# Layer 1's normalization: channel sums added on GpSimd, steps begun a quarter earlier, one turned tile in another PSUM pool

## The chip, the cores and the metric

The kernel runs on one core of one Trainium2 chip. The time is device microseconds of one execution, as the median of several runs. A core has five engines with a queue each: TensorE (PE, matmuls; PEld are its weight loads), VectorE (DVE), ScalarE (ACT), GpSimd (POOL) and SyncE (SP, which here issues most DMAs). Matmul results land in PSUM and are moved to SBUF by VectorE or ScalarE.

## The reference

Four layers follow each other on an image batch of 8 x 56 x 56 x 192; each adds a block to its input after a group normalization. The change is inside layer 1, a shifted window attention:

```python
mu = jnp.mean(x, axis=-1, keepdims=True)
var = jnp.var(x, axis=-1, keepdims=True)
x = (x - mu) * jax.lax.rsqrt(var + EPS) * gamma + beta      # over the 192 channels of a token
sx = jnp.roll(x, shift=(-3, -3), axis=(1, 2))
win = ...                                                   # 8 x 8 windows of 7 x 7 = 49 tokens
qkv = (win @ w_qkv + b_qkv)...
attn = softmax(q * scale @ k.T + bias + mask)               # 6 heads
out = (attn @ v) @ w_proj + b_proj
```

What is changed is how the two sums over channels come about, of x and of x squared for every token, from which mean and variance follow.

## The kernel before

Channels lie on partitions: an image is a tile of 128 partitions (two halves of the rows, 64 channels each) by 3 channel blocks by pixels. Layer 1 goes through 8 images (b), and each image in four **quarters** (g): 7 rows of each half, 16 windows. A quarter is one turn of the loop over g, and its work is written out by hand in one string, `plan`, whose letters are taken in turn. VectorE, ScalarE, GpSimd and TensorE keep exactly that order (`manual_schedule`); an engine's instruction waits in its queue until the one ahead of it is done.

- X: exponentials of the scores (ScalarE, L928), Y: their sums and reciprocals (VectorE, L933, L934) and the product with them (GpSimd, L935); one X and one Y for each half, called X0, X1, Y0, Y1 below.
- T: the shares turned by TensorE in three tiles of 128 x 512 for each half (L956), copied to SBUF by ScalarE (first and third, L961) and VectorE (second, L963).
- P: shares times values (L971), with two PSUM tiles, and the copies of the result (L980, L981).
- R: the output projection (L990, L997), added to the image by VectorE (L1004). G: statistics for layer 2 (L1007).
- Q (three times) and V (twice): queries, keys and values of the next quarter (L886, L901); ScalarE evacuates Q's first half (L890) behind the X ahead of it, and the first values (L906).
- E: scores of the next quarter (L916), the mask added and the maximum taken by VectorE (L921, L923), the maximum subtracted by GpSimd (L924); E0 and E1 for the halves.
- N: one step of the generator `layer1_norm` for the next image. There are 13 in a quarter, called N1 to N13 below.

```python
plan = "X Q N Y V N X G Q N Y N T T T P N V N N T T T P G Q N R N E N R N G E N R N".split()
```

`layer1_norm` clears the gaps of the window tile `xr` (L782, L783), then, for each of four tiles of 16 windows, copies the image scaled by the group normalization into window order with eight GpSimd instructions, two a step (`windows`, L805), and squares it with two ScalarE instructions (`squares`, L812). For two tiles at a time a burst of matmuls with a matrix of 1/192 sums x (L844) and its squares (L848) over channels into one PSUM tile of the pool `mm`; ScalarE squares the mean (L855), VectorE subtracts (L859). After both halves come the floor (L818), Ln (L820) and Exp (L822), `finish`, and for each tile `scaled`: a matmul that spreads the factor over partitions (L827) and two VectorE products (L832). That is 33 steps, begun in quarter 0 of an image for the next image; `run(steps)` ahead of quarter 3 takes whatever is left, since quarter 3 is the first that reads the next image's `xr`. The windows' copies fall in N1 to N8 and the squares in N9 to N12 of quarters 0 and 1, each burst of sums in N13, and `finish` and `scaled` in N1 to N7 of quarter 2. Quarter 3 has no step.

PSUM: the pool `mm` has three banks, used by Q, V, R's first half, the sums, L827 and the third turned tile; the pool `et` has two, for the first two turned tiles, P and R's second half.

Image data for image b + 2 is loaded by SyncE in quarters 1 to 3 of image b (L761): rows of quarter 0 first, of quarters 1 and 2 next, of quarter 3 last.

Of the kernel before, what the change touches and what calls it, by code (L numbers as in the profile page):

```python
# [10 lines left out]
F32 = mybir.dt.float32  # L11
AF = mybir.ActivationFunctionType
ALU = mybir.AluOpType
# [76 lines left out]
def kernel(ctx: ExitStack, tc: tile.TileContext, a: dict, out: bass.AP):  # L90
# [681 lines left out]
    def in_pairs(z):  # L772
        return z.rearrange("p (k z t) -> p k z t", z=2, t=WN)

    def layer1_norm(b, x, pool, psum, consts, first=False):


        ones32, sel = consts[4:]
        xr = pool.tile([128, XR], F32, name="xr")
        blocks = xr[:, 0:12 * GW].rearrange("p (g j n) -> p g j n", j=3, g=4)  # L780
        pads = xr[:, 0:12 * GW].rearrange("p (a n) -> p a n", n=PW)
        nc.gpsimd.memset(pads[:, :, WN:64], 0.0)  # L782
        nc.gpsimd.memset(xr[:, 12 * GW:], 0.0)  # L783
        rs = pool.tile([128, TT], F32, name="rs1", bufs=1)
        msq = pool.tile([128, TT], F32, name="msq", bufs=1)
        yield xr
        sc, sh = scsh1[:, 0, b:b + 1], scsh1[:, 1, b:b + 1]

        def windows(g):

            xg = x[:, :, 7 * g:7 * g + 7]
            copies = []
            for j in range(3):
                for z, nw in ((0, 4), (1, 3)):
                    dst = blocks[:, g, j].rearrange("p (k n) -> p k n", n=PW)[:, 0:nw, 64 * z:64 * z + WN]
                    src = xg[:, j, :, 3 + 28 * z:3 + 28 * z + 7 * nw].rearrange("p i (w j) -> p w i j", j=7)
                    copies.append((dst.rearrange("p k (i j) -> p k i j", j=7), src))
            last = blocks[:, g, :, 3 * PW + 64:3 * PW + 64 + WN].rearrange("p c (i j) -> p c i j", j=7)
            copies += [(last[:, :, :, 0:4], xg[:, :, :, 52:56]), (last[:, :, :, 4:7], xg[:, :, :, 0:3])]
            for n, (dst, src) in enumerate(copies):  # L800
                if first and n % 3 == 1:
                    nc.scalar.activation(dst, src, AF.Identity, bias=sh, scale=sc)
                else:
                    eng = nc.vector if first and n % 3 == 2 else nc.gpsimd
                    eng.tensor_scalar(dst, src, sc, sh, ALU.mult, ALU.add)  # L805
                if n % 2:
                    yield

        def squares(g, sq):
            for z in range(2):  # L810
                src = blocks[:, g].rearrange("p c (k n) -> p c k n", n=PW)[:, :, :, 64 * z:64 * z + WN]
                nc.scalar.activation(  # L812
                    sq[:, z].rearrange("p c (k t) -> p c k t", t=WN), src, AF.Square
                )
                yield

        def finish(rows):
            nc.vector.tensor_scalar(rs[rows], rs[rows], 0.0, 1e-5, ALU.max, ALU.add)  # L818
            yield
            nc.scalar.activation(rs[rows], rs[rows], AF.Ln)  # L820
            yield
            nc.scalar.activation(rs[rows], rs[rows], AF.Exp, scale=-0.5)  # L822
            yield

        def scaled(g):
            bp = psum.tile([128, 512], F32, name="rstd", tag="mm", bufs=3)[:, 0:TT]
            nc.tensor.matmul(bp, sel[32 * g:32 * g + 32], rs[32 * g:32 * g + 32], start=True, stop=True)  # L827
            for z in range(2):
                xs = blocks[:, g].rearrange("p c (k n) -> p c k n", n=PW)[:, :, :, 64 * z:64 * z + WN]
                by = bp[:, 4 * WN * z:4 * WN * (z + 1)].rearrange("p (k t) -> p k t", t=WN)  # L830
                by = by.unsqueeze(1).to_broadcast([128, 3, 4, WN])
                nc.vector.tensor_tensor(xs, xs, by, ALU.mult)  # L832

        for g0, n in ((0, 1), (1, 1), (2, 2)) if first else ((0, 2), (2, 2)):
            sqs = []
            for g in range(g0, g0 + n):
                yield from windows(g)
            for g in range(g0, g0 + n):
                sqs.append(pool.tile([128, 2, 3, 4 * WN], F32, name="sq", bufs=2))
                yield from squares(g, sqs[-1])  # L840
            ps = psum.tile([128, 512], F32, name="stat", tag="mm", bufs=3)
            for j in range(3):
                for k in range(n):
                    nc.tensor.matmul(  # L844
                        in_pairs(ps[32 * k:32 * k + 32, 0:TT]), ones32, in_slots(xr, (3 * (g0 + k) + j) * GW),
                        start=(j == 0), stop=(j == 2),
                    )
                    nc.tensor.matmul(  # L848
                        ps[64 + 32 * k:96 + 32 * k, 0:TT].rearrange("p (z n) -> p z n", z=2), ones32, sqs[k][:, :, j],
                        start=(j == 0), stop=(j == 2),  # L850
                    )
            rows = slice(64, 64 + 32 * n)
            for z in range(2):
                src = in_pairs(ps[0:32 * n, 0:TT])[:, :, z]
                nc.scalar.activation(  # L855
                    msq[rows, 4 * WN * z:4 * WN * (z + 1)].rearrange("p (k t) -> p k t", t=WN), src, AF.Square
                )
            to = slice(32 * g0, 32 * (g0 + n))
            nc.vector.tensor_tensor(rs[to], ps[rows, 0:TT], msq[rows], ALU.subtract)  # L859
            yield  # L860
            if first:
                yield from finish(to)
                for g in range(g0, g0 + n):
                    scaled(g)
                    yield
        if first:
            return
        yield from finish(slice(0, 128))
        for g in range(4):
            scaled(g)  # L870
            yield
# [70 lines left out]
    def layer1_mix(g, x, v, pool, psum, es, consts, st):  # L942
# [6 lines left out]
        def turn(s, i):  # L949

            e, et = es[g % 2][s], ets[s]
            tag, bufs = ("mm", 3) if i == 2 else ("et", 2)
            tp = psum.tile([128, 512], F32, name="et_ps", tag=tag, bufs=bufs)
            for k in range(4):
                at = 8 * i + 2 * k
                nc.tensor.transpose(  # L956
                    tp[:, 128 * k:128 * k + 128], e[:, at:at + 2].rearrange("p a b -> p (a b)"), ident
                )
            dst = et[:, 4 * i:4 * i + 4].rearrange("p a b -> p (a b)")
            if i % 2 == 0:  # L960
                nc.scalar.copy(dst, tp)  # L961
            else:
                nc.vector.tensor_copy(dst, tp)  # L963
# [509 lines left out]
    with ExitStack() as st:  # L1473
# [37 lines left out]
        ))  # L1511
        last = slice(nimg - 1, nimg)
        gn, stats = [], []
        for b in range(nimg):
            gn.append(pool.tile([128, 3, NTH, 6], F32, name="gh_st"))
            steps = iter(())
            if b + 1 < nimg:
                steps = layer1_norm(b + 1, x[b + 1], pool, psum, consts)
                xr.append(next(steps))
            for g in range(4):  # L1520
                if g == 1 and b + 2 < nimg:
                    x.append(layer1_image(xpool))
                if g and b + 2 < nimg:
                    for piece in ((), (0,), (1, 2), (3,))[g]:
                        rolled(x1[b + 2], x[b + 2], piece, False)
                if g == 1 and b == 0:
                    run(gn_finish(mv1[:, last], scsh1[:, 0, last], scsh1[:, 1, last], pool, psum, "mm"))
                if g == 1 and b:
                    gn_aggregate(gn[b - 1], mv2[:, b - 1])
                if g == 1 and b == nimg - 1:  # L1530
                    run(gn_finish(mv2[:, 0:b], scsh2[:, 0, 0:b], scsh2[:, 1, 0:b], pool, psum, "mm"))
                if g == 3:
                    run(steps)
                parts, now = layer1_mix(g, x[b], values, pool, psum, es, consts, gn[b])
                parts.update(softmax, G=stats)
                if g < 3 or b + 1 < nimg:
                    values, of_next, softmax = layer1_scores((g + 1) % 4, xr[b + (g == 3)], pool, psum, S, es, consts)
                    parts.update(of_next)
                for kind in plan:
                    if kind == "N":  # L1540
                        next(steps, None)
                    elif parts.get(kind):
                        parts[kind].pop(0)()
                stats = now
                rolled(x2[b], x[b], g, True)
# [231 lines left out]
```

## Time and profile before

| | us |
|---|---|
| median of 3 runs | 5501.04 (5497.55 to 5502.83) |
| the profiled execution | 5505.7, of which the span 5503.9 |
| layer 1's loop, from the first X0 to the last | 924.4 (2001.3 to 2925.7 of the span) |
| of it busy: TensorE | 839.1 |
| VectorE | 620.0 |
| ScalarE | 392.0 |
| GpSimd | 379.3 |

The page gives the span, busy times by engine and groups of instructions. A timeline line gives start, length, engine, line, operation, operands and a count; in square brackets stands how long the engine was idle before it and which engine, tile and line ended that. A window line gives, for a stretch of the span, the busy time of each engine (with instruction counts), the share of TensorE's full clock that was granted (PEclk), and DMA traffic. TensorE works a float32 matmul in two passes, which the profile counts as two records.

### The profile page before, as it was taken

What the parts mean: (1) busy time and instruction counts of PE and PEld (TensorE: products, weight loads), DVE (VectorE), ACT (ScalarE), POOL (GpSimd) and SP (SyncE); (2) the same over time, 40 slices, a digit from 0 to 9 for tenths busy, and PEclk for the clock granted to TensorE, in tenths of its full rate; (3) what the DMA queues carried; (4) which work ended last, traced back from release to release, by engine and by line L of the source; (5) the groups of instructions that cost most, each with busy time, mean ns of one, the idle gap of its engine ahead of it and who ended that gap; (6) DMA issues with size and microseconds to landing.
All of it is one profiled execution on the core that took longest, in us unless ns stands there. A gap on an engine that the chain in (4) does not pass through costs nothing. (4 is left out here: it accounts for less than half of the span.)

```text
span 5503.9 us, 113538 instructions
## 1 busy us (share of the span) xinstructions
PE 4998.8 (91%) x49428; PEld 3379.9 (61%) x49428; DVE 3053.1 (55%) x4273; ACT 2311.1 (42%) x3109; POOL 1877.9 (34%) x1583
## 2 busy tenths in 40 slices
PE   7999969999999979999987989998798787999999
PEld 6778866666666645666665757775344586444444
DVE  4555533555555456666666868888777214343331
ACT  3444435555555434444441025554576302333333
POOL 5555555555555434344431023333011101001000
PEclk9999989999999989999998999999899898999999
DMA  5989896777777623223225757675777696212211
GB/s 148 234 222 232 222 269 261 272 273 275 277 276 272 201 68 85 77 81 86 82 59 156 270 214 235 230 237 188 182 218 220 241 340 235 65 61 87 70 40 27
DMA packets 533335, 1002.87 MB, mean 182 GB/s; under 512 B 256104, under 2 KB 467812, under 8 KB 501460
## 3 DMA queue, kind: packets, MB, share of 16 engines
q1 hardware_dynamic: 519984, 945.58, 53.5%
q0 software_dynamic: 8576, 40.69, 2.3%
q10 hardware_dynamic: 4276, 9.32, 0.6%
q8 instruction: 389, 6.37, 0.5%
q14 instruction: 110, 0.90, 0.1%
HBM read 665.22 MB, written 346.75 MB: 184 GB/s over the span
## 5 line engine op out<-in xcount | busy, mean ns | idle before, releaser
L465 POOL COPY lc<-lt 128x896 f32<-128x896 f32 (+1 forms) x320 | 616.4, 1934 | 513.9 <-PE op L473 490.7
L432 PE MATMUL qv<-w_qv_sb,x 64*112 64x256 f32 (+1 forms) x5376 | 692.0, 410 | 24.0 <-DVE act L438 20.1
L432 PEld LDWEIGHTS qv<-w_qv_sb,x 64*112 64x112 f32 x5376 | 592.5, 176 | 112.5 <-DVE act L438 32.2
L438 DVE TENSOR_TENSOR act<-qv,b_qv 112x640 f32<-112x640 f32 x448 | 318.7, 752 | 325.4 <-PE qv L432 238.5
L442 ACT ACTIVATE act<-act 112x640 f32<-112x640 f32 x448 | 300.3, 683 | 414.3 <-DVE act L438 403.7
L408 POOL TENSOR_TENSOR qv<-act 112x320 f32<-112x320 f32 x448 | 346.5, 799 | 288.9 <-ACT act L442 193.6
L473 PEld LDWEIGHTS op<-rc,lc 128*56 128x56 f32 x9216 | 329.6, 135 | 124.2 <-issue 65.9
L1366 PE MATMUL ph<-y,w_sb 64*128 64x392 f32 x2304 | 398.9, 499 | 6.5 <-ACT hid L1370 6.5
L473 PE MATMUL op<-rc,lc 128*56 128x56 f32 x9216 | 354.5, 221 | 55.1 <-ACT rc L465 38.2
L1377 PE MATMUL po<-hid,w_sb 128*64 128x392 f32 x2304 | 386.3, 494 | 0.0
L1384 DVE TENSOR_TENSOR x<-x,z 128x392 f32<-128x392 f32 x96 | 72.8, 759 | 520.3 <-ACT z L1382 520.3
L1097 PE MATMUL cv<-zc,wt 128*128 128x224 f32 x1536 | 312.8, 355 | 24.9 <-DMA zc<-pd 24.2
L1097 PEld LDWEIGHTS cv<-zc,wt 128*128 128x128 f32 x1536 | 290.3, 189 | 68.3 <-issue 53.1
L1366 PEld LDWEIGHTS ph<-y,w_sb 64*128 64x128 f32 x2304 | 220.7, 189 | 176.5 <-issue 26.5
L506 PE MATMUL y<-pp,w_o_sb 128*64 128x392 f32 x1536 | 309.0, 499 | 5.8 <-DVE pp L500 5.8
L1112 POOL TENSOR_TENSOR rows<-rows,loc 128x896 f32<-128x896 f32 x96 | 223.3, 2326 | 261.9 <-ACT rows L1108 204.6
L483 PE MATMUL pj<-xn,w_p_sb 64*128 64x392 f32 x1536 | 289.1, 509 | 19.7 <-ACT pp L490 18.1
L924 POOL TENSOR_TENSOR e<-e,mx 128x1176 f32<-128x1176 f32 x64 | 140.2, 2190 | 462.6 <-DVE mx L923 398.3
L465 ACT COPY rc<-rt 128x896 f32<-128x896 f32 (+1 forms) x160 | 279.9, 1749 | 40.0 <-DMA rt<-right 40.0
L1377 PEld LDWEIGHTS po<-hid,w_sb 128*64 128x64 f32 x2304 | 162.7, 137 | 213.8 <-issue 213.8
L500 DVE TENSOR_TENSOR pp<-pp,ot 128x784 f32<-128x784 f32 x128 | 124.1, 970 | 292.6 <-PE ot L495 239.9
L1115 DVE TENSOR_TENSOR_SCAN sums<-dec,rows 64x896 f32<-64x896 f32 x96 | 278.5, 2901 | 1.3
(252 smaller groups left out, 9194.8 us busy)
## 6 DMA issues: line engine op xcount, KB each, us to landing
lt<-left SPq DMA_DIRECT2D x72, 1792.0 KB
rt<-right SPq DMA_DIRECT2D x72, 1792.0 KB
left<-qv SPq DMA_DIRECT2D x224, 252.0 KB
right<-qv SPq DMA_DIRECT2D x96, 504.0 KB
wt<-in_band_dram SPq DMA_DIRECT2D x23, 2048.0 KB
zc<-pd SPq DMA_DIRECT2D x187, 232.0 KB
pd<-pt SPq DMA_DIRECT2D x7, 5568.0 KB
bm<-bmask SPq DMA_DIRECT2D x64, 588.0 KB
```

Of the source, the lines that this page charges most:

```text
L408: nc.gpsimd.tensor_tensor(qv[:, s, s0:s1, k], *(acts[s][:, which, 0:n].rearrange("p (s d) -> p s d", d=64) for which in range(2)), ALU.mult,)
L432: nc.tensor.matmul(ps[s][:, which, 0:n], x[64 * s:64 * s + 64, j, bass.ts(i, 2 * W)], w_qv[64 * s:64 * s + 64, j, which, 64 * s0:64 * s1], ...
L438: nc.vector.tensor_tensor(acts[s][:, :, 0:n], ps[s][:, :, 0:n], b_qv[:, :, 64 * s0:64 * s1], ALU.add)
L442: nc.scalar.activation(acts[s][:, :, 0:n], acts[s][:, :, 0:n], AF.Silu)
L465: copy(c[:, 0:nu], raw.rearrange("p (w u d) -> p u d w", u=nu, d=64 // nu)[:, :, d0:d0 + 8])
L473: nc.tensor.matmul(op[64 * u:64 * u + W, i, :], lc[:, u, i], rc[:, u, i], start=True, stop=True)
L483: nc.tensor.matmul(ps[:, s, 0:TT], w_p[64 * s:64 * s + 64, j, 128 * c:128 * c + 128], xn[64 * s:64 * s + 64, j, bass.ts(t, TT)], start=(j ...
L506: nc.tensor.matmul(y[64 * s:64 * s + 64], w_o[:, 2 * g + u, 64 * j:64 * j + 64], pp[:, u, s], start=(u == 0), stop=(u == 1),)
L1097: nc.tensor.matmul(dst, wt[:, c4 + i, 128 * q:128 * q + 128], zc[:, :, c4 + i, q:q + NPAIR], start=(q == 0), stop=(q == 1),)
L1115: nc.vector.tensor_tensor_scan(_reversed(sums[0:64]), d[0:64], _reversed(rows[0:64]), 0.0, ALU.mult, ALU.add)
L1366: nc.tensor.matmul(ps[:, s, 0:TT], w0[64 * s:64 * s + 64, j, m * 128:(m + 1) * 128], y[64 * s:64 * s + 64, j, ts], start=(j == 0), stop=(j ...
L1377: nc.tensor.matmul(ps[64 * s:64 * s + 64], w1[:, m, 64 * j:64 * j + 64], hid[:, m, s], start=(m == 0), stop=(m == 5),)
```

## The change

In `layer1_norm`, for all images but the first, GpSimd adds the three channel blocks of x (tile `xs`, two additions for each of the four tiles) and of the squares (in place in `sq`, two additions), so that one matmul instead of three sums each of them. Empty steps (`yield`) are put in. The generator then has 45 steps. Each image's steps begin in quarter 3 of the image before the one in which they began so far; for image 1 they begin where they did. In `turn` the second turned tile takes a bank of `mm` in place of one of `et`. In the changed kernel the lines behind `layer1_norm` stand 34 lower (X is L962, Q L920, V L935, T L990, P L1005), and the additions are L882, L883 and L887, the sums L892 and L895.

```diff
-        for g0, n in ((0, 1), (1, 1), (2, 2)) if first else ((0, 2), (2, 2)):
...
+        def variance(ps, g0, n):
             rows = slice(64, 64 + 32 * n)
...
+        if first:
+            for g0, n in ((0, 1), (1, 1), (2, 2)):
...
             return
+
+        for g0 in (0, 2):
+            tiles = []
+            for g in (g0, g0 + 1):
+                sq = pool.tile([128, 2, 3, 4 * WN], F32, name="sq", bufs=2)
+                xs = pool.tile([128, 4, 2, WN], F32, name="xs", bufs=2)
+                tiles.append((xs, sq))
+                yield from windows(g)
+                nc.gpsimd.tensor_tensor(xs, in_slots(xr, 3 * g * GW), in_slots(xr, (3 * g + 1) * GW), ALU.add)
+                nc.gpsimd.tensor_tensor(xs, xs, in_slots(xr, (3 * g + 2) * GW), ALU.add)
+                yield from squares(g, sq)
+                yield
+                for j in (1, 2):
+                    nc.gpsimd.tensor_tensor(sq[:, :, 0], sq[:, :, 0], sq[:, :, j], ALU.add)
+                yield
+            yield
+            ps = stat()
+            for k, (xs, sq) in enumerate(tiles):
+                nc.tensor.matmul(
+                    ps[32 * k:32 * k + 32, 0:TT], ones32, xs.rearrange("p k z t -> p (k z t)"), start=True, stop=True
+                )
+                nc.tensor.matmul(
+                    halves(ps[64 + 32 * k:96 + 32 * k, 0:TT]), ones32, sq[:, :, 0], start=True, stop=True
+                )
+            variance(ps, g0, 2)
+            yield
         yield from finish(slice(0, 128))
+        yield
+        yield
         for g in range(4):
             scaled(g)
             yield
...
-            tag, bufs = ("mm", 3) if i == 2 else ("et", 2)
+            tag, bufs = ("mm", 3) if i else ("et", 2)
...
+        def normalize(b):
+            if b >= nimg:
+                return iter(())
+            steps = layer1_norm(b, x[b], pool, psum, consts)
+            xr.append(next(steps))
+            return steps
+
+        steps = normalize(1)
         for b in range(nimg):
             gn.append(pool.tile([128, 3, NTH, 6], F32, name="gh_st"))
-            steps = iter(())
-            if b + 1 < nimg:
-                steps = layer1_norm(b + 1, x[b + 1], pool, psum, consts)
-                xr.append(next(steps))
...
                 if g == 3:
                     run(steps)
+                    steps = normalize(b + 2)
```

The steps fall as follows, for images 2 to 7. Quarter 3: copies of tile 0 (N1 to N4), its additions and squares (N5, N6, N8), copies of tile 1 (N9 to N12), its first additions and first square (N13). Quarter 0: its second square and last additions (N1, N3), the sums of tiles 0 and 1 (N5), copies of tile 2 (N6 to N9), its additions and squares (N10, N11, N13). Quarter 1: the same for tile 3 in N1 to N8, the sums of tiles 2 and 3 (N10), `finish` (N11 to N13). Quarter 2: `scaled` (N3 to N6).

More of the change, by code (lines that the diff above doesn't have):

```diff
@@ L832, in scaled @@
                 nc.vector.tensor_tensor(xs, xs, by, ALU.mult)
-        for g0, n in ((0, 1), (1, 1), (2, 2)) if first else ((0, 2), (2, 2)):
[L835 to L851, printed above, removed]
+        def variance(ps, g0, n):
             rows = slice(64, 64 + 32 * n)
@@ L859, in layer1_norm @@
             nc.vector.tensor_tensor(rs[to], ps[rows, 0:TT], msq[rows], ALU.subtract)
-            yield
-            if first:
+            return to
+        stat = lambda: psum.tile([128, 512], F32, name="stat", tag="mm", bufs=3)
+        halves = lambda z: z.rearrange("p (z n) -> p z n", z=2)
+        if first:
+            for g0, n in ((0, 1), (1, 1), (2, 2)):
+                sqs = []
+                for g in range(g0, g0 + n):
+                    yield from windows(g)
+                for g in range(g0, g0 + n):
+                    sqs.append(pool.tile([128, 2, 3, 4 * WN], F32, name="sq", bufs=2))
+                    yield from squares(g, sqs[-1])
+                ps = stat()
+                for j in range(3):
+                    for k in range(n):
+                        nc.tensor.matmul(
+                            in_pairs(ps[32 * k:32 * k + 32, 0:TT]), ones32, in_slots(xr, (3 * (g0 + k) + j) * GW),
+                            start=(j == 0), stop=(j == 2),
+                        )
+                        nc.tensor.matmul(
+                            halves(ps[64 + 32 * k:96 + 32 * k, 0:TT]), ones32, sqs[k][:, :, j],
+                            start=(j == 0), stop=(j == 2),
+                        )
+                to = variance(ps, g0, n)
+                yield
                 yield from finish(to)
@@ L865, in layer1_norm @@
                     yield
-        if first:
             return
+        for g0 in (0, 2):
[4 more added lines that the diff above has]
+                tiles.append((xs, sq))
+                yield from windows(g)
+                nc.gpsimd.tensor_tensor(xs, in_slots(xr, 3 * g * GW), in_slots(xr, (3 * g + 1) * GW), ALU.add)
[6 more added lines that the diff above has]
+            yield
+            ps = stat()
+            for k, (xs, sq) in enumerate(tiles):
+                nc.tensor.matmul(
+                    ps[32 * k:32 * k + 32, 0:TT], ones32, xs.rearrange("p k z t -> p (k z t)"), start=True, stop=True
+                )
+                nc.tensor.matmul(
+                    halves(ps[64 + 32 * k:96 + 32 * k, 0:TT]), ones32, sq[:, :, 0], start=True, stop=True
+                )
+            variance(ps, g0, 2)
+            yield
         yield from finish(slice(0, 128))
+        yield
+        yield
         for g in range(4):
```

## The prediction

> **What bounds the kernel now.** Section 1 of the page has TensorE busy 91%. Then the busy time by window, over quarters 0 to 3 of image b = 4, which the others repeat:
>
> ```profile
> core 0: us, PE busy (x) PEld busy (x) DVE busy (x) ACT busy (x) POOL busy (x), PEclk, DMA share, GB/s
> 2486.10:2514.20 28.10, 26.26 (x564) 17.35 (x560) 19.69 (x34) 14.08 (x24) 16.91 (x22) 1.00 0.28 77
> 2514.20:2542.70 28.50, 26.90 (x565) 17.52 (x564) 19.33 (x34) 14.03 (x25) 16.26 (x20) 1.00 0.59 144
> 2542.70:2576.60 33.90, 29.90 (x555) 19.86 (x556) 23.53 (x41) 12.04 (x20) 8.76 (x4) 0.95 0.18 54
> 2576.60:2602.70 26.10, 24.09 (x542) 16.84 (x540) 17.76 (x31) 10.98 (x18) 8.75 (x4) 1.00 0.25 71
> ```
>
> TensorE sets the pace, and quarter 2, with `finish` and `scaled`, costs 7.8 us over quarter 3. TensorE's timeline shows what stops it (two lines of quarter 2, then quarter 3):
>
> ```profile
> 2552.28 0.92 PE L827 MATMUL rstd<-rs,sel 32*128 32x392 f32 x2 [2.19 <-ACT rs L822]
> 2553.13 2.34 PE L956 MATMUL et_ps<-ident,e 128*128 128x128 f32 x12
> ...
> 2575.48 2.25 PE L886 MATMUL qk_ps<-xr,wg 64*128 64x392 f32 x12
> 2578.36 2.32 PE L901 MATMUL v_ps<-wg,xr 64*128 64x192 f32 x24 [0.62 <-DVE x L1004]
> 2580.41 2.97 PE L886 MATMUL qk_ps<-xr,wg 64*128 64x392 f32 x12
> 2583.31 1.53 PE L956 MATMUL et_ps<-ident,e 128*128 128x128 f32 x12
> 2585.63 0.27 PE L971 MATMUL po<-et,v 49*32 49x49 f32 x2 [0.80 <-ACT et L961]
> 2586.26 1.20 PE L971 MATMUL po<-et,v 49*32 49x49 f32 x94 [0.36 <-DVE et L963]
> ```
>
> I count from the quarter's first Q (2575.48 = 0): T starts at 7.83. See the wait of 2.19 for Exp, and that T then takes 2.34, not 1.53. GpSimd and ScalarE at the edge to the next quarter (Q at 2601.64):
>
> ```profile
> 2581.05 2.19 POOL L935 TENSOR_TENSOR e<-e,sm 128x1176 f32<-128x1176 f32 x1 [0.74 <-DVE sm L934]
> 2585.81 2.19 POOL L935 TENSOR_TENSOR e<-e,sm 128x1176 f32<-128x1176 f32 x1 [2.57 <-DVE sm L934]
> 2600.52 2.19 POOL L924 TENSOR_TENSOR e<-e,mx 128x1176 f32<-128x1176 f32 x1 [12.53 <-DVE mx L923]
> 2604.55 2.19 POOL L924 TENSOR_TENSOR e<-e,mx 128x1176 f32<-128x1176 f32 x1 [1.83 <-DVE mx L923]
> ```
>
> ```profile
> 2602.75 1.21 ACT L928 ACTIVATE e<-e 128x1176 f32<-128x1176 f32 x1 [6.32 <-POOL e L924]
> 2603.97 0.59 ACT L890 ACTIVATE qk<-qk_ps,bq 128x392 f32<-128x392 f32 x1
> ```
>
> Y0's product ends at 7.76, just when T can start: GpSimd has no slack there. X0 starts as E0's subtraction ends (2602.71), and Q's evacuation stands right behind X0. Prices, by line and shape:
>
> ```profile
> L805 POOL TENSOR_SCALAR xr<-x,scsh 128x196 f32<-128x196 f32 x83 | 43.1, 519 | 0.4
> L812 ACT ACTIVATE sq<-xr 128x588 f32<-128x588 f32 x56 | 34.8, 692 | 0.3
> L832 DVE TENSOR_TENSOR xr<-xr,rstd 128x588 f32<-128x588 f32 x60 | 45.1, 765 | 14.0 <-PE rstd L827 12.7
> ```
>
> [...] 2.19 us idle were enough for half clock in quarter 2 (PEclk 0.95, T 0.8 us longer). [...] the sums' four strips start within 20 ns of each other and come again every 0.33 us. [...]
>
> **The change part by part.**
>
> *Sums.* A burst held TensorE from 2511.42 to 2513.54, 2.1 us for 24 passes in six groups of four. Eight passes are two groups, 0.36 + 0.33, with the turn-over 0.8 us. 14 bursts save 18 us, all on TensorE's path.
>
> *Additions.* 16 an image of 392 elements. Nearest row L924: 1.86 ns an element, 0.73 us; dearest, L408 (865 ns for 320), 1.06. I take 0.85, 1.7 for a pair.
>
> *Loads.* SyncE's order does not change. The copies' rows were issued a quarter or more ahead, and landings take 5.2 to 9.5 us: nothing waits. The clearing of `xr` waits for the last Q of quarter 2, long done.
>
> *Quarter 3 (so far empty).* Clearing (0.83) and N1's copies (1.05) now stand ahead of Y0 on GpSimd, as in quarter 0 so far, where T waited 1.00. GpSimd: E1's subtraction ends 4.8, Y0 6.7 to 8.9, N2 and N3 to 11.0, Y1 to 13.2, N4 to 14.1. The square in N5 waits for N4's copies, and in the built order ScalarE's copies of V and of the second T stand behind it: square 14.8, V 15.3, second square 16.0, T's copy 16.6. The second P starts at 16.6, not 15.5. Quarter 27.1 after 26.2: **+0.9**.
>
> *Quarter 0.* The first square of tile 1 (N13 of quarter 3) stands ahead of X0 on ScalarE and waits for N12's copies. These stand behind E1's subtraction on GpSimd. From Q: E0's subtraction ends 1.1, N10 and N11 3.2, E1's subtraction 5.4, N12 6.25, square 7.0, X0 8.2, Q's evacuation 8.8 (so far 2.9). The second Q takes that bank in the built order, and its other half waits for the first V's copy, behind the copy of k (0.84) and another square (0.69): 10.8, so far 5.65. TensorE loses 5.2; nothing behind is early enough to take it up. With the sums (0.8) and 0.2 from the turned tile: 26.2 + 5.2 + 0.8 - 0.2 = 32.0 after 28.1. An idle time twice that of quarter 2 brings half clock; one slice of 3.4 us costs 1.7. **+5.6**.
>
> *Quarter 1.* N13's additions (1.7) and N1's copies put Y0 at 7.7 to 9.9; T waits 2.1, of which P's waits give back 1.1. Then the squares hold the second P as in quarter 3. 28.8 with the sums, after 28.5: **+0.3**.
>
> *Quarter 2.* Exp is long done: 2.19 gone. Next is VectorE: `scaled` 0 and 1, four products of 0.765, now stand ahead of T1's copy, with Y1's reduction between. That copy ends at 14.2, P's second third waits 2.7, the second P ends at 22.4, so far 24.1, and the tail is 0.3 shorter: **-2.0**. Half clock as before.
>
> *Turned tile.* P's second matmul no longer waits for L963's copy (0.36), but passes that had waited ran faster (94 in 1.20, unhindered 96 in 1.6): 0.2 a quarter. The third tile now needs Q's bank, free by then.
>
> *Image 1.* Three quarters only, so four `scaled` come in one piece ahead of quarter 3: 3.2 of matmuls, 6.1 of VectorE, Q's banks held until products 1 and 2 are done: V some 7.9 late. By quarter: -1.2, +5.4, -4.7, +7.7 = +7.2.
>
> Sum: 6 x (0.9 + 5.6 + 0.3 - 2.0) = 28.8, image 1 +7.2, five last quarters -1.0: **+35 us**, span 5539. The profiled execution is 4.7 over the median; I add 35 to the median: **5536**.
>
> **The rivals.**
> 1. *Faster:* the end of `finish` decides. Place: quarter 2. If T1's copy is not late and no half clock follows, quarter 2 falls from its mean of 35.1 (six images; 33.4 to 38.4) to 31.5, -3.6; with X0 gated by N11 alone (3.4 us earlier, 1.8 lost, no half clock) quarter 0 is +0.5. 6 x (0.9 + 0.5 + 0.3 - 3.6) = -11, image 1 +2, last -1: 5491. It decides once quarter 0 loses less than about 2.4. For it: the 2.19 is the longest regular stall. Against: the built order has the square's wait on the last copy.
> 2. *Much slower:* additions at 1.06 and half clock for two slices in quarter 0 and one in quarter 1 (T's wait of 2.1 is near the 2.19): +4.2 an image and +3: 5564. For: half clock lasted 17 us once (quarter 2 of image 3, PEclk 0.78).
> 3. *The early start does not come about* (a late load or a held buffer stalls GpSimd, and with it the softmax). Each us is lost in full, 7 times; 2 us give 5550. Against: the landings above.
>
> **How the numbers follow.** Forecast 0.70 (own range 5513 to 5554: half clock absent or double, additions at both ends), rival 1 0.14, rival 2 0.13, rival 3 0.03. The range 5500 to 5565 leaves out most of rival 1 and the far end of rival 2. The 0.2% that a measurement of this kernel can tell is 11 us. Faster 0.11 from rival 1; same 0.07 from its slow end and the forecast's low end; slower 0.82.
>
> **What would show it.** ScalarE's first exponential of each quarter 0 some 6 us behind E0's subtraction, with the square ending just before it and GpSimd named as its releaser; TensorE idle some 5 us ahead of the second Q there, PEclk below 1; bursts of 0.8 us; no 2.19 ahead of L827; a wait of P for VectorE in quarter 2; additions of 0.73 to 1.06. Wrong, if X0 follows E0 within 3 us in quarter 0, or if quarter 2 falls to 31 or less.

## The result, and the profile after

| | before | after |
|---|---|---|
| median of the runs, us | 5501.5 (6 runs) | 5542.2 (6 runs) |
| ratio to before, with its 95% interval | | 1.0071 (1.0058 to 1.0084) |
| span of the profiled execution, us | 5503.9 | 5540.5 |
| layer 1's loop, from the first Q of image 0's quarter 1 to that of image 7's quarter 2, us | 858.7 | 909.2 |
| GpSimd busy in the loop, us | 379 | 485 |

The change makes the kernel 0.7% slower, 40.7 us by the medians, where 35 were forecast. In the profiled executions the loop is 50.5 us longer. Outside it, where nearly all of the code is the same, this execution was some 14 us shorter: its first stage alone ended 8.8 us sooner, before anything that was changed. Such differences come without a cause in the change: over the profiled executions of this text's eleven kernels the time outside the loop lies between 4631 and 4646 us. So the forecast's total fits better than its terms, and the terms are what the experiments are about.

A quarter is measured from its first Q to the next one's. The four quarters that the prediction worked through, of the same image, in the view of windows of the kernel after (start and end, length, then the busy time of TensorE, its weight loads, VectorE, ScalarE and GpSimd with instruction counts, the granted share of TensorE's clock, and DMA):

```profile
2602.77:2629.70 26.93, 24.34 (x544) 16.90 (x541) 18.33 (x32) 12.06 (x20) 18.39 (x21) 1.00 0.25 71
2629.70:2661.83 32.13, 27.34 (x552) 17.94 (x548) 18.29 (x33) 13.78 (x24) 18.76 (x23) 0.95 0.19 55
2661.83:2690.59 28.76, 24.75 (x552) 16.87 (x548) 19.05 (x34) 12.62 (x22) 20.99 (x21) 1.00 0.60 154
2690.59:2729.17 38.58, 33.36 (x552) 22.82 (x548) 25.55 (x42) 11.90 (x20) 8.32 (x5) 0.82 0.16 48
```

These are quarters 3, 0, 1 and 2. Quarter 0 and quarter 2 are the long ones, and they are the two with a clock below 1. The means over images 1 to 6 (quarter 3: 1 to 5), with the size that the prediction gave each:

| quarter | before | after | measured | predicted |
|---|---|---|---|---|
| 3 | 26.4 | 26.9 | +0.4 | +0.9 |
| 0 | 28.5 | 32.5 | +3.9 | +5.6 |
| 1 | 28.6 | 29.1 | +0.6 | +0.3 |
| 2 | 34.9 | 37.9 | **+3.0** | **-2.0** |

Image 0's four quarters, in the first three of which image 1 is normalized, rose by 5.4 us together (predicted 7.2): by 0.5, 0.6, 3.6 and 0.7 us (predicted -1.2, +5.4, -4.7 and +7.7).

Quarter 0 goes in its mechanism as the prediction said. ScalarE and GpSimd of the kernel after, in the timeline (start, length, engine, line, operands; in brackets the idle time before and what ended it); Q starts at 2629.70:

```profile
2635.49 0.70 ACT L812 ACTIVATE sq<-xr 128x588 f32<-128x588 f32 x1 [11.37 <-POOL xr L805]
2636.09 1.19 ACT L962 ACTIVATE e<-e 128x1176 f32<-128x1176 f32 x1
2637.18 0.57 ACT L924 ACTIVATE qk<-qk_ps,bq 128x392 f32<-128x392 f32 x1
```

```profile
2628.16 2.19 POOL L958 TENSOR_TENSOR e<-e,mx 128x1176 f32<-128x1176 f32 x1 [6.00 <-DVE mx L957]
2630.33 2.17 POOL L805 TENSOR_SCALAR xr<-x,scsh 128x196 f32<-128x196 f32 x4
2632.47 2.19 POOL L958 TENSOR_TENSOR e<-e,mx 128x1176 f32<-128x1176 f32 x1
2634.64 0.82 POOL L805 TENSOR_SCALAR xr<-x,scsh 128x84 f32<-128x84 f32 x2
2635.54 1.02 POOL L882 TENSOR_TENSOR xs<-xr 128x392 f32<-128x392 f32 x1
2636.64 0.95 POOL L883 TENSOR_TENSOR xs<-xs,xr 128x392 f32<-128x392 f32 x1
2639.24 2.19 POOL L969 TENSOR_TENSOR e<-e,sm 128x1176 f32<-128x1176 f32 x1 [1.66 <-DVE sm L968]
```

E0's subtraction (the first L958) ends at 2630.35, and X0 (L962) could start there. It starts at 2636.09, behind the square L812, which waits for copies that stand behind E1's subtraction. In the loops of both traces no instruction of ScalarE, VectorE or GpSimd starts more than 0.12 us ahead of the end of the one before it. TensorE pays:

```profile
2637.80 0.92 PE L920 MATMUL qk_ps<-xr,wg 64*128 64x392 f32 x2 [2.12 <-ACT qk L924]
2639.75 3.62 PE L920 MATMUL qk_ps<-xr,wg 64*128 64x392 f32 x10 [1.03 <-ACT v L940]
```

The second of these Q's took 3.62 us for ten passes, where the quarter's first Q took 2.25 us for twelve; the granted clock over the 3.62 us is 0.60, half clock for 2.9 of them. (Passes are the records: the one matmul of L827 in `scaled` stands as x2 in every timeline here.)

Quarter 2 does not go as predicted. TensorE in the timeline of the kernel after, from Q at 2690.59:

```profile
2694.81 3.90 PE L935 MATMUL v_ps<-wg,xr 64*128 64x192 f32 x24 [1.97 <-DVE x L1038]
...
2704.11 0.63 PE L990 MATMUL et_ps<-ident,e 128*128 128x128 f32 x4 [0.62 <-DVE xr L832]
2704.67 0.55 PE L1005 MATMUL po<-et,v 49*32 49x49 f32 x32
2707.67 0.90 PE L1005 MATMUL po<-et,v 49*32 49x49 f32 x64 [2.45 <-DVE et L997]
2708.50 1.49 PE L827 MATMUL rstd<-rs,sel 32*128 32x392 f32 x2
2709.91 4.21 PE L935 MATMUL v_ps<-wg,xr 64*128 64x192 f32 x24
```

The 2.19 us for Exp are gone, and P's wait for VectorE is there (2.45 us, predicted 2.7). But V waits 1.97 us for VectorE ahead of that, which the prediction does not have, and V then takes 3.90 and 4.21 us where it takes 2.22 at full clock. The granted clock, 0.905 in the mean of the six quarters 2 before, is 0.84 after. In the loops of both traces the clock stands at half for stretches of 3.41 us or two to five times that. The six quarters 2 have 12 times 3.41 us before and 22 times after; at most half of each is lost, by which I estimate 3.4 us a quarter before and 6.3 after. This difference, 2.8 us, is nearly the 3.0 by which quarter 2 rose. TensorE's idle time rose too, from 3.9 to 5.2 us, and its other busy time fell by about as much.

### The profile page after: what moved, and what is told of

It reads as the page before. It is cut to its first block, busy times and chain, and to the rows that moved or that the text cites. A ratio compares the mean times of both kernels' runs of the same rounds, so it can differ in the third digit from the quotient of the medians.

```text
span 5540.5 us, 113218 instructions
## 1 busy us (share of the span) xinstructions
PE 4999.7 (90%) x49204; PEld 3390.4 (61%) x49204; DVE 3059.2 (55%) x4273; ACT 2305.6 (42%) x3109; POOL 1982.4 (36%) x1695
## 5 line engine op out<-in xcount | busy, mean ns | idle before, releaser
L1327 POOL TENSOR_TENSOR yl<-yl,dwb 128x1344 f32<-128x1344 f32 (+1 forms) x40 | 86.4, 2182 | 549.2 <-DMA yl<-yd 549.2
L958 POOL TENSOR_TENSOR e<-e,mx 128x1176 f32<-128x1176 f32 x64 | 140.2, 2190 | 397.2 <-DVE mx L957 356.7
```

## The experiments

Two theories stood after this. One: the loss lies in *where* steps stand in the queues, a square ahead of X0 and VectorE's work ahead of V's bank and of T's copy, each made dearer by half clock. The other: it lies in GpSimd's load, 112 additions of 1.0 us. The first four kernels take them apart. Each is compared with the kernel before; all values are medians and means of quarters from the profile.

| kernel | time, us | ratio to before, 95% | quarter 0 | 1 | 2 | 3 |
|---|---|---|---|---|---|---|
| before (beside these runs) | 5498 to 5499 | | 28.5 | 28.6 | 34.9 | 26.4 |
| after | 5542.2 | 1.0058 to 1.0084 | 32.5 | 29.1 | 37.9 | 26.9 |
| turn_alone | 5475.1 | 0.9945 to 0.997 | 28.0 | 27.9 | 33.3 | 25.8 |
| square_later | 5525.5 | 1.0032 to 1.0059 | 29.2 | 29.3 | 37.0 | 26.8 |
| scaled_later | 5519.9 | 1.0032 to 1.0057 | 32.9 | 29.3 | 33.4 | 26.8 |
| no_adds | 5537.1 | 1.0054 to 1.0082 | 34.2 | 30.1 | 34.6 | 26.4 |
| all_later | 5488.7 | 0.9972 to 0.9985 | 29.1 | 29.0 | 30.7 | 26.9 |
| all_later_no_adds | 5479.6 | 0.9945 to 0.9973 | 28.3 | 30.5 | 30.2 | 26.6 |
| turn_scaled | 5462.3 | 0.992 to 0.9945 | 28.0 | 27.8 | 30.5 | 25.8 |
| adds_behind_y | 5463.2 | 0.9917 to 0.9943 | 26.9 | 27.7 | 30.7 | 26.9 |
| adds_behind_y_image1 | 5458.0 | 0.9908 to 0.9935 | 26.9 | 27.4 | 30.7 | 26.6 |

### turn_alone: the turned tile by itself

On the kernel before:

```diff
-            tag, bufs = ("mm", 3) if i == 2 else ("et", 2)
+            tag, bufs = ("mm", 3) if i else ("et", 2)
```

> The kernel before with nothing but the second turned tile in a bank of mm. Theory from the after trace (quarters without any step of the normalization lost 1.2 us and 0.5 us): about 0.5 us a quarter over 31 quarters, some -16 us, so near 5485. The prediction's own term was 0.2 us a quarter, -6 us, near 5495. Rival: the bank of mm is missed by Q, V or R, and the quarters lengthen: 5505 or more.

Measured 5475.1, 24 us below before, with an interval from 16 to 30; the loop is 16.5 us shorter. Every quarter gained 0.5 to 0.7 us, and quarter 2 gained 1.5. In quarter 2, P's later wait for VectorE's copy, 1.51 us in six of seven images before, is 0.9 us or less here. TensorE's P of a quarter 0 in the timeline, before:

```profile
2612.26 0.27 PE L971 MATMUL po<-et,v 49*32 49x49 f32 x2
2612.70 1.20 PE L971 MATMUL po<-et,v 49*32 49x49 f32 x94 [0.16 <-DVE et L963]
...
2617.44 1.61 PE L971 MATMUL po<-et,v 49*32 49x49 f32 x96
```

and of turn_alone:

```profile
2594.45 1.33 PE L971 MATMUL po<-et,v 49*32 49x49 f32 x96
...
2599.32 1.31 PE L971 MATMUL po<-et,v 49*32 49x49 f32 x96
```

From the first T to the V behind the first P it is 3.01 us before and 2.72 here, and 3.00 and 2.70 for the second half. The prediction took 1.6 us for an unhindered P. It was the second half's, which shows no wait in brackets and yet was held up; unhindered it is 1.3. So this part is worth 0.6 us a quarter and not 0.2, and 1.5 in quarter 2. No new wait of Q, R or V for the bank of `mm` shows. Set against turn_alone, the rest of the change costs some 65 us, and 4.6 us in quarter 2 (37.9 after 33.3).

### square_later: the square behind X0

```diff
                 yield from windows(g)
...
-                yield from squares(g, sq)
-                yield
+                if g == 1:
+                    yield
+                    yield
+                    steps = squares(g, sq)
+                    next(steps)
+                    yield
+                    next(steps)
+                else:
+                    yield from squares(g, sq)
+                    yield
```

> The changed kernel, with the first square of tile 1 put off by two steps, from behind the last R of quarter 3 to behind X0, Q and V of quarter 0, and the second square by two; nothing else moves. Theory (ScalarE's queue: X0 stands behind a square that waits for GpSimd's copies): X0 of quarter 0 starts within 1.5 us of E0's subtraction, the second Q no longer waits, quarter 0 falls from 32.3 us to 28 to 29, six times, so -20 to -25 us against the changed kernel: 5517 to 5522. Rival (it is GpSimd's load, 98 us more in the loop, that makes quarter 0 long, through a late Y0): quarter 0 stays above 31 and T waits for GpSimd by 2 us or more; 5535 or more.

Measured 5525.5, 17 us below after (the theory gave 5517 to 5522); quarter 0 fell by 3.3 us to 29.2, just over the 28 to 29 put. X0 follows E0's subtraction at once. But a second wait came up that the first had hidden. TensorE in quarter 0 of square_later:

```profile
2627.42 2.97 PE L928 MATMUL qk_ps<-xr,wg 64*128 64x392 f32 x12
2632.66 2.65 PE L998 MATMUL et_ps<-ident,e 128*128 128x128 f32 x12 [2.27 <-POOL e L977]
```

The second Q has no wait any more, and T waits 2.27 us for Y0's product on GpSimd. So the queue of ScalarE is the cause of most of quarter 0's loss, as predicted; the rival's sign, T waiting for GpSimd by over 2 us, is there as well. What that wait costs, adds_behind_y shows further down: another 2.2 us.

### scaled_later: the products behind T's copy

```diff
         yield from finish(slice(0, 128))
-        yield
-        yield
+        for _ in range(4):
+            yield
         for g in range(4):
```

> The changed kernel with four empty steps in place of two ahead of scaled, so that all its VectorE products stand behind the copy of the second turned tile in quarter 2. Theory 1 (P waits 2.45 us for that copy because of four products ahead of it, and the long half clock follows from this wait): the wait goes, the half clock of 10.3 us goes, quarter 2 falls from 37.9 us to 33 to 34, six times -24 to -29: about 5515. Theory 2 (the late finish and sums at the edge of quarter 1 hold E1's subtraction and so V and X0, and the half clock comes from there): only the 2.45 us go, or less; quarter 2 stays at 35.5 or more: 5528 or more.

Measured 5519.9, 22 us below after, with quarter 2 at 33.4. By the sizes this is theory 1. Yet V's wait is still there, and half clock behind it in five of six images. TensorE of scaled_later, quarter 2:

```profile
2684.37 3.35 PE L935 MATMUL v_ps<-wg,xr 64*128 64x192 f32 x24 [1.97 <-DVE x L1038]
2687.51 3.21 PE L920 MATMUL qk_ps<-xr,wg 64*128 64x392 f32 x12
2690.65 1.53 PE L990 MATMUL et_ps<-ident,e 128*128 128x128 f32 x12
2692.97 1.52 PE L1005 MATMUL po<-et,v 49*32 49x49 f32 x96 [0.80 <-ACT et L995]
```

P's wait fell from 2.45 to 0.80, which took 4.5 us from the quarter. What is left comes from theory 2's place: in the one quarter where V waited 1.72 us and no half clock followed, quarter 2 was 31.2; the other five lie between 32.8 and 34.9. So both theories hold a part. Waits of 1.72 and 1.97 us ended differently here; the last section shows that the length of a wait alone does not decide.

### no_adds: the steps where they are, without the additions

```diff
-                nc.gpsimd.tensor_tensor(xs, in_slots(xr, 3 * g * GW), in_slots(xr, (3 * g + 1) * GW), ALU.add)
-                nc.gpsimd.tensor_tensor(xs, xs, in_slots(xr, (3 * g + 2) * GW), ALU.add)
...
-                for j in (1, 2):
-                    nc.gpsimd.tensor_tensor(sq[:, :, 0], sq[:, :, 0], sq[:, :, j], ALU.add)
...
```

The sums are again the 24 passes of the kernel before.

> The changed kernel with every step where it is, but without GpSimd's additions: the sums again as 24 passes in bursts of 2.1 us. If the loss lies in where the steps stand (the squares ahead of X0, the products ahead of T's copy), taking the additions away gives back only the bursts' 18 us and at most some 4 us at quarter 1: +10 to +18, near 5555. If it lies in GpSimd's load of 1.0 us for each of 112 additions, quarters 0 and 1 fall by 2 to 4 us each, more than the bursts cost, and the kernel is faster than the changed one: 5530 or less.

Measured 5537.1, 5 us below after and in between what the two theories gave; the two intervals overlap, so the total decides nothing. The quarters do. Quarters 0 and 1 did not fall by 2 to 4 us, as the load theory had it; they are longer by 1.7 and 0.9, where bursts of 2.1 us in place of 0.8 alone make 1.3 each. Quarter 1 is a sum of more: T's wait of 2.4 us for Y0 is gone, and in four of six images TensorE stands 1.3 to 1.8 us ahead of P with no releaser in the profile, with half clock behind it in three. Quarter 2 is *shorter* by 3.3, though nothing in it was changed. The start of quarter 2 of no_adds:

```profile
2699.73 2.25 PE L918 MATMUL qk_ps<-xr,wg 64*128 64x392 f32 x12
2702.69 2.22 PE L933 MATMUL v_ps<-wg,xr 64*128 64x192 f32 x24 [0.72 <-DVE x L1036]
```

V waits 0.72 us in place of 1.97, which is 1.25 less: what the longer burst at the end of quarter 1 takes. At that edge VectorE is late, and the time that the short burst saves TensorE is handed back as a longer wait for VectorE. Half clock follows that wait in five of six images of after; here V takes its 2.22 us. P's wait of 2.45 us is in both kernels; no_adds has 12 times 3.41 us of half clock in its six quarters 2, as many as before, and after has 22. VectorE of the kernel after at this edge (V waits for the last line's end):

```profile
2688.73 0.57 DVE L842 TENSOR_TENSOR rs<-stat,msq 64x392 f32<-64x392 f32 x1
2689.33 0.88 DVE L1038 SCALAR_TENSOR_TENSOR x<-pr,bpr,x 128x196 f32<-128x196 f32 x3
2690.12 1.06 DVE L818 TENSOR_SCALAR rs<-rs 128x392 f32<-128x392 f32 x1
2691.11 0.56 DVE L1041 BATCH_NORM_STATS2 gh_st<-x 128x6 f32<-128x392 f32 x1
2691.59 1.36 DVE L955 TENSOR_TENSOR e<-S,bm 128x1176 f32<-128x1176 f32 x1
2693.05 1.38 DVE L957 TENSOR_REDUCE mx<-e 128x24 f32<-128x1176 f32 x1
2694.34 0.86 DVE L1038 SCALAR_TENSOR_TENSOR x<-pr,bpr,x 128x196 f32<-128x196 f32 x3
```

It runs without a gap, so each instruction in it counts. The variance (L842) and the floor of `finish` (L818), 1.6 us together, are what the change put in; before, both came after the third R's addition.

### all_later: the three moves together

square_later's edit, and:

```diff
+        if b > 1:
+            for _ in range(3):
+                yield
         yield from finish(slice(0, 128))
-        yield
         yield
         for g in range(4):
```

> The changed kernel with three moves: the squares of tile 1 behind X0, Q and V of quarter 0; finish in the first three steps of quarter 2 instead of the last three of quarter 1 (not for image 1); scaled in the four steps behind the first P of quarter 2. Theory (finish in VectorE's queue, its floor of 1.06 us above all, delays the third R's addition, and with it V's bank, at the edge to quarter 2): V's first wait falls from 1.97 us to about 0.9, the half clock there goes, quarter 2 falls from the 33.4 us of scaled_later to about 31, quarter 0 stays at the 29.2 us of square_later; -55 to -61 against the changed kernel, 5481 to 5487. Rival (it is the shorter burst alone that brings V to its bank too early): V's wait stays near 2 us, quarter 2 at 33 to 34, and the total is the sum of the two single moves, about -40: near 5502.

Measured 5488.7, 53 us below after and 10 us below before; quarter 2 is 30.7 in the mean, with a granted clock of 1.00 in all six images. TensorE of all_later, quarter 2, has no long wait left:

```profile
2653.44 2.22 PE L945 MATMUL v_ps<-wg,xr 64*128 64x192 f32 x24 [0.99 <-DVE x L1048]
2655.50 2.97 PE L930 MATMUL qk_ps<-xr,wg 64*128 64x392 f32 x12
2659.61 1.53 PE L1000 MATMUL et_ps<-ident,e 128*128 128x128 f32 x12 [1.15 <-POOL e L979]
2661.13 1.26 PE L1015 MATMUL po<-et,v 49*32 49x49 f32 x96
2662.32 0.92 PE L827 MATMUL rstd<-rs,sel 32*128 32x392 f32 x2
```

V's wait fell by 0.98 us, the floor's place in VectorE's queue; that, with the half clock that it tipped, was 2.7 us a quarter (33.4 to 30.7). The theory's size was nearly met (-53 for -55 to -61), the rival's was not.

### all_later_no_adds: what the additions are worth there

The same edit as no_adds, on all_later.

> As all_later, but the sums again as 24 passes in bursts of 2.1 us, without GpSimd's additions. If the additions cost nothing in a good place, 1.3 us a burst come back: +18 against all_later. If a burst's 1.3 us in quarter 1 only let TensorE arrive sooner at a wait for VectorE, as the 0.72 us of V's wait in no_adds against 1.97 us in the changed kernel suggests, and the additions hold Y0 and with it T in quarter 0 by 2.3 us, then quarters 0 and 1 fall by the additions as much as they rise by the bursts: within 6 us of all_later, or faster than it.

Measured 5479.6, some 9 us *below* all_later; the loops are within 1 us of each other (the intervals of the totals touch. Here its quarters 1 are long, four of six with a clock of 0.94 or 0.95: in these four TensorE stands 1.4 to 2.5 us ahead of P with no releaser in the profile, and what sets that off stays open). So the additions, which remove 18 us of bursts, still bring nothing that shows. A reason shows in T's wait, in TensorE's timeline of quarters 1, first of all_later:

```profile
2631.39 1.87 PE L1000 MATMUL et_ps<-ident,e 128*128 128x128 f32 x12 [2.41 <-POOL e L979]
```

and then of all_later_no_adds:

```profile
2627.99 1.53 PE L998 MATMUL et_ps<-ident,e 128*128 128x128 f32 x12 [0.25 <-POOL e L977]
```

In quarters 0 they are 2.28 us and none in the same image. Two additions, 2.0 to 2.1 us together, stand ahead of Y0's product on GpSimd in each.

### adds_behind_y: the same additions behind Y1

On all_later, with the loop over tiles written out (`add_x` and `add_sq` are the two additions of a tile's channel blocks and of its squares, `sums` the burst):

```diff
         yield from windows(1)
         yield
         yield
         yield from tile()
+        add_x(1)
+        add_sq(1)
         yield
         w = windows(2)
         for _ in range(3):
             next(w)
             yield
+        sums(0)
...
         yield from windows(3)
         z = tile()
+        add_sq(2)
         add_x(3)
```

> As all_later, with the additions that stood ahead of Y0 on GpSimd moved: those of tile 1 behind Y1 of quarter 0 (with the sums of tiles 0 and 1 three steps later), those of tile 2's squares behind Y1 of quarter 1. Theory (an addition costs nothing but where it stands ahead of Y0, since T waits for Y0's product: 2.27 and 2.41 us in all_later, 0.15 and 0.25 us without additions): T's waits in quarters 0 and 1 fall by 2 us each, and the loop by 24 to 28 us: 5461 to 5465, 15 us or more below all_later_no_adds. Rival (GpSimd is too full: the additions now hold the sums, the copies or E1's subtraction instead): the wait turns up there, and the time stays at 5475 or more.

Measured 5463.2, 25 us below all_later and 16 us below all_later_no_adds. T in quarter 1 of adds_behind_y:

```profile
2614.54 1.53 PE L1033 MATMUL et_ps<-ident,e 128*128 128x128 f32 x12 [0.35 <-POOL e L1012]
```

GpSimd does the same work, and the 2.4 us are gone. Theory met in the time and in T's waits; the loop fell by 21 us, a little less than the 24 to 28 put. No cost of GpSimd's load as such shows here; four of its 16 additions for an image stood in the wrong place.

### adds_behind_y_image1: image 1 without a rest

On adds_behind_y, image 1 with the steps of the kernel before and one empty one:

```diff
+        if b == 1:
...
+            yield from finish(slice(0, 128))
+            yield
+            for g in range(4):
+                scaled(g)
+                yield
+            return
```

> As adds_behind_y, with image 1, which has three quarters for its steps and not four, normalized as in the kernel before (24 passes a burst, 33 steps and one empty one), so that none of its scaled is left over to be done in one piece ahead of quarter 3. Theory: image 0's three quarters fall from 93.6 us to the 87.0 us of turn_scaled, -6 to -7 us against adds_behind_y: near 5456, below turn_scaled. Rival: the piece ahead of quarter 3 is hidden: no difference.

Measured 5458.0, 5 us less, which the intervals do not separate. Image 0's last three quarters fell from 91.7 to 86.6 us, and the loop by 8.6. That is near what the theory put on the four `scaled` done in one piece. But the edit also takes image 1's additions and short bursts out, and it is one image in one execution, so the cause is not isolated.

### turn_scaled: the small version

On turn_alone:

```diff
         yield from finish(slice(0, 128))
+        yield
         for g in range(4):
```

> The kernel before with the turned tile in the bank of mm and one empty step ahead of scaled, so that the first of its matmuls stands behind the first P of quarter 2 and not ahead of the turned tiles. Theory: the wait of 2.19 us for Exp goes, with it the half clock behind it, and quarter 2 falls from 33.3 us (turn_alone) to 30.5 to 31, seven times 2.3 to 2.8: 5455 to 5460. Rival: the last two products now stand ahead of R's additions on VectorE, which bounds the last third of a quarter, and give 1.5 us back: 5466 or more.

Measured 5462.3, 13 us below turn_alone and 37 us (0.7%) below before. Quarter 2 is 30.5 with a clock of 1.00. The theory gave 5455 to 5460, the rival 5466 or more; the quarter says theory (its products ahead of R's additions did not lengthen it), the total lies between.

The fastest kernel, adds_behind_y_image1, is 0.8% below before (ratio 0.9908 to 0.9935), but turn_scaled, two lines away from before and with neither additions nor an early start, has 0.992 to 0.9945. The intervals overlap: what the additions and the early start bring, each in its best place found here, can't be told from nothing. By quarters, the larger kernel gains 1.2 and 0.4 us in 0 and 1, where bursts shorter by 1.3 us stand, and gives back 0.8 and 0.2 in 3 and 2.

## Why the prediction was right, and where it was not

*Quarter 0 (+5.6, measured +3.9).* The mechanism is as put: square ahead of X0, copies behind E1's subtraction, second Q late. Moving the square alone gave back 3.3 of it. Three terms were off. Q's evacuation ended 8.05 us behind the quarter's Q and not 8.8, and the second Q's other half started at 10.05 and not 10.8: by the prediction's own count TensorE lost 4.4 us there and not 5.2. Something behind did take part of it up: T's wait of 1.00 us for Y0, which the quarter had before, is gone. And the turned tile gave 0.6 and not 0.2. One slice of half clock was right: a clock of 0.95 over 32 us, which is one stretch of 3.41 us. The 1.7 put for it was the author's estimate, half of 3.4; of the ten stretches in the loop of before, eight are 3.41 us long. Not in the prediction: T's wait of 2.3 us for Y0, which the late second Q hid and square_later laid bare.

*Quarter 2 (-2.0, measured +3.0): the step that failed.* "2.19 gone" is right, and so is P's wait (2.7 put, 2.45 measured). "Half clock as before" is wrong: what it can have cost went from 3.4 to 6.3 us. The term that is missing is V's wait of 1.97 us at the edge: the floor and the variance moved into VectorE's unbroken queue ahead of the third R's addition were put at nothing, and so was TensorE's earlier arrival there. That is the rule which the prediction applied to ScalarE in quarter 0, not applied to VectorE. no_adds divides the error: with V's wait at 0.72 us and P's at 2.45, half clock is as before, as put, and quarter 2 is 34.6 us long. So 3.3 of the 5.0 us between the forecast and the measurement came with V's wait. The other 1.7 were not taken apart; of the 2.0 put as a gain, 0.3 came, although the turned tile alone gave 1.5.

*Sums (18 us "all on TensorE's path").* A burst is 0.8 us, as put. At the edge to quarter 2, 1.25 us of its 1.3 came back as a wait (0.72 in no_adds, 1.97 after). There, TensorE arrived sooner at a wait and saved next to nothing.

*Quarter 3 (+0.9, measured +0.4).* Without the turned tile (0.7 in turn_alone) it is +1.1; the prediction's own +0.9 with 0.2 taken off is the same +1.1. *Quarter 1 (+0.3, measured +0.6):* T's wait 2.41 for 2.1; right. The one long image of the six (31.2 us) has a wait of 2.5 us with no releaser in the profile; the other five give +0.15.

*Additions (0.85, measured 1.03, 0.95 and 1.02).* Within the bounds given (0.73 to 1.06), at their upper end. Where they stood mattered far more than their size.

*Image 1 (+7.2, measured +5.4).* The sum is near, its parts are not: the +7.7 put in quarter 3 is 0.7, and quarter 2, put at -4.7, is +3.6. One image in one execution tells little, too: turn_alone, which leaves image 1's steps alone, has image 0's last three quarters at 94.2 us, above the 93.1 of after (88.2 before), with a clock of 0.77 in quarter 2. adds_behind_y_image1 points to the four `scaled` in one piece, but does not show them to be the cause.

*The rivals.* Rival 1, faster, needed quarter 2 at 31.5 and X0 hardly late in quarter 0. all_later gave it 30.7 and 29.1 and ended below before: the rival was a real kernel, three moves away. Rival 2's dear additions and more half clock came in part: more half clock, but in quarter 2.

The forecast was right in sign and within 6 us of the median. That closeness is luck, two errors against each other: over six images quarter 2 was 30 us too low, quarters 0 and 3 and image 1 some 15 us too high, and the rest of the program came out shorter in the profiled execution.

## What to carry over

Where engines keep a written order, ask of every instruction that a change moves what stands *behind* it in that queue: a 0.7 us square cost 3.3 us a quarter, two additions of 2 us together cost about 2 us each time, and some steps further on neither held TensorE. Work shortened ahead of a wait for another engine can come back as wait (1.25 of a burst's 1.3 us at the edge to quarter 2), so follow the saving to the next wait before booking it. And where the profile shows half clock behind waits of some 2 us, price the next such wait as a chance of half clock and not as a certainty, and compare kernels over many quarters: V's wait of 1.97 us had half clock behind it in five of six quarters 2 of after and in two of six of square_later.

## What the runs showed of the hardware

*VectorE's floor took three times as long beside a subtraction on GpSimd.* The floor L818 (128x392) takes 353 or 354 ns in each of its seven executions on 128 partitions in the loop of the kernel before, where GpSimd is idle, and 1061 or 1062 ns in each of the kernel after. In the timeline of after, GpSimd's subtraction runs across it:

```profile
2688.78 2.19 POOL L958 TENSOR_TENSOR e<-e,mx 128x1176 f32<-128x1176 f32 x1 [7.08 <-DVE mx L957]
```

It ends at 2690.97; the floor started at 2690.12 and ended at 2691.18, 0.2 us behind it. In all seven of after, a subtraction that had started first ran across the floor, and the floor ended 0.2 us behind it. In all_later, where the subtraction lies otherwise, the floor takes 1.32 us at 2539.79 (the median of the line is 1316 ns) and again ends 0.2 us behind GpSimd's, which runs from 2538.70 to 2540.89. So 0.7 of the 1.06 us at that edge were there only with GpSimd beside it; what holds the floor was not shown.

*Half clock came behind 3.41 us with TensorE half idle, not behind a wait of a given length.* Within the loops of before and after the granted clock changes 63 times, and in each trace all changes lie within 2 ns of one grid, 3.413 us wide. Two waits of the kernel after show what stood ahead of half clock. In quarter 1, T waits 2.41 us for Y0:

```profile
2672.42 1.53 PE L990 MATMUL et_ps<-ident,e 128*128 128x128 f32 x12 [2.41 <-POOL e L969]
```

No half clock follows. Behind V's shorter wait of 1.97 us in quarter 2 it does. These are grid windows, the first two around T's wait, then one with V's wait and one with P's of 2.45 us (the second number after the window is TensorE's busy time, the third from the end the clock):

```profile
2667.77:2671.18 3.41, 2.24 (x11) 1.05 (x10) 2.11 (x5) 2.18 (x3) 3.23 (x5) 1.00 1.01 302
2671.18:2674.59 3.41, 2.17 (x70) 2.00 (x73) 1.77 (x3) 1.59 (x3) 3.21 (x6) 1.00 1.01 231
2691.66:2695.07 3.41, 1.44 (x10) 0.64 (x8) 3.31 (x6) 2.18 (x4) 0.50 (x1) 1.00 0.30 84
2705.31:2708.73 3.42, 1.06 (x65) 0.99 (x66) 2.33 (x5) 0.16 (x2) 2.19 (x1) 1.00 0.00 0
```

T's wait is shared by two windows, each busy for over 2 us. V's and P's lie in one window each, busy for 1.44 and 1.06 us, and half clock starts at its end. Counted over the grid windows at full clock in the loops of before and after, half clock followed 23 of 23 with TensorE busy for less than 1.6 us, 8 of 14 with 1.6 to 2.0 us, and none of 427 with more. And one and the same wait ended either way: the 2.19 us for Exp had half clock behind it in seven of seven quarters 2 before, while in turn_alone two of six quarters 2 have a clock of 1.00; V's 1.97 us had it in five of six in after and in two of six in square_later.

Nor did one busy window end it every time. The next three windows of the kernel after:

```profile
2708.73:2712.14 3.41, 3.41 (x16) 2.31 (x17) 2.20 (x4) 0.43 (x2) 0.00 (x0) 0.50 0.02 5
2712.14:2715.55 3.41, 3.41 (x16) 1.97 (x12) 0.56 (x1) 0.48 (x1) 0.00 (x0) 0.50 0.00 0
2715.55:2718.96 3.41, 3.41 (x47) 2.97 (x52) 2.23 (x3) 1.03 (x2) 0.00 (x0) 0.50 0.00 0
```

TensorE is busy without a gap, and the clock stays at half for 10.2 us. Of 46 windows at half clock with TensorE busy for 3.3 us or more, in the same two loops, 14 were followed by another at half. In all 14, L827's matmuls (32*128 in the timeline) had 0.5 us or more of the window; of the other 32, which were followed by full clock, 3 had that. Whether these matmuls are the reason was not tried.
